# Norm roots as exp(-0.5 ln) on ScalarE instead of a power on GpSimd, and another rule for which products go to GpSimd

## The chip, the cores and the metric

The kernel runs on one core of one Trainium2 chip. The metric is device time in microseconds of one execution; the time before is the median of three runs, 29434.43 us (29426.01 to 29453.37). The engines are named as the profile names them: PE is TensorE, DVE is VectorE, ACT is ScalarE, POOL is GpSimd, SP issues all DMAs.

## What is computed

Eight images of 64 channels and 128 x 128 pixels, in fp32, pass a softmax-weighted 3x3 filter (layer 0) and then a block that holds a two-layer, two-directional state-space scan and a gated feed-forward (layer 1). Cut to what matters here:

```python
def layernorm(x, w, b):                      # rmsnorm: the same without the mean
    mu = x.mean(-1, keepdims=True)
    var = ((x - mu) ** 2).mean(-1, keepdims=True)
    return (x - mu) * jax.lax.rsqrt(var + EPS) * w + b

def selective_scan(u, dt, A, Bm, Cm, D, z):
    dt = jax.nn.softplus(dt)
    dA = jnp.exp(jnp.einsum('bdl,dn->bldn', dt, A))
    dBu = jnp.einsum('bdl,bnl,bdl->bldn', dt, Bm, u)
    # hs[l] = dA[l] * hs[l-1] + dBu[l], along l = 128*128 tokens
    y = jnp.einsum('bldn,bnl->bdl', hs, Cm) + D[None, :, None] * u
    return y * jax.nn.silu(z)

x_norm = ln4d(input, norm1_w, norm1_b)       # over the 64 channels
seq = layernorm(tokens(x_norm), pe_norm_w, pe_norm_b)
for i in range(2):                           # two directions in each
    seq = bimamba_block(seq, ...)            # begins with an rmsnorm
x = input + dw * x_mamba                     # dw: 1x1 and depthwise 3x3 of x_norm
xn = ln4d(x, norm2_w, norm2_b)
g1, g2 = split(depthwise3x3(ffn_in @ xn))
return x + ffn_out @ (jax.nn.gelu(g1, approximate=False) * g2)
```

The scan has 128 channels x 16 states per direction, so it is by far the largest part.

## The kernel before

**Tiling.** The scans of all images, layers and directions are cut into 512 chunks of 1024 tokens (64 per image: 16 for each of two directions in each of two layers). A chunk has 16 *units* (U); a unit is one tile of 128 (channel, state) pairs by 1024 tokens. Units go in pairs k, whose order is in `PAIRS`.

**One unit.** `decay` (L1112) makes w = exp(dt * A) on ScalarE into one of two PSUM buffers. `drive` (L1107) makes bu = dt*u*B on GpSimd, 2048 columns for a pair, in three buffers. `scan` (L1122) runs the recurrence on VectorE. `product` (L1151) multiplies by C, either on GpSimd or on VectorE. `keep` (L1148) copies the last column to `state` on ScalarE. `collect` (L1162) adds over states on PE, once per pair, and gives the pair's hs buffer (one of three) free. Where the product is made is decided by `on_pool` (L1095): if it is GpSimd, the scan writes to hs in SBUF and the product follows one unit later; if it is VectorE, the scan writes in place into w and the product reads it from there.

```python
def on_pool(self, u):
    if u % 2 or u % 8 == 4 or self.t0 + u - 1 in gelu_times:
        return False
    return u != 8 or self.beside_front or self.beside_gelu
```

**Order.** There is no scheduler at run time: `at(time, phase, fn)` (L396) files every step under a time, counted in units, and one of six phases (FEED, SCAN, MID, PROD, DECAY, REST), and the program is written out in that order, each engine keeping it. Chunk i has its scans at times 16i to 16i+15; its projections come up to two chunks earlier, its norm (second direction only) in the chunk after.

**Background stages.** Beside the scans of one image, other steps run on the same engines: *fronts* of the next image (`Front.plan`, L648: filter, three norms n1, n2, n3, every 24 units), *mix* of the image before (`Mix.plan`, L752: two 3x3 convolutions and one norm, every 13 units) and *feed-forward* of the image before (`Ffn.plan`, L912: three GELUs every 24 units). In a cycle of 64 chunks, mix lies beside chunks 0 to 11 (it starts beside chunk 62), feed-forward beside 12 to 34, fronts beside 36 to 63. Image 0 has its own first fronts partly ahead of all scans (a prologue of 514 us) and then beside its first 12 chunks; no mix or feed-forward runs beside image 0. Image 7 has no fronts beside it, and its own mix starts beside its chunk 51; its own feed-forward stands alone after the last scan.

**A norm.** `means` (L469) sums squares on PE into PSUM, 8 columns. `means_out` (L473) copies them to `r` on ScalarE and adds eps. `root` (L477) raises `r` to the power -0.5 on GpSimd. `spread` (L480) broadcasts the roots over the channels on PE into a bank `rb`, which VectorE multiplies by (L609, L641, L1221). Each step has its own time in `plan`: in Front, `means_out` of n1 and `root` stand at a + 26, `spread` at a + 28, the multiplication at a + 29.

**Tables.** [...] `silu` (L1012), `softplus` (L1039) and `gelus` (L868) each use a set of their own; `decay` and the softmax use Exp. Loads of tables are put in by the compiler just ahead of the instruction that needs them, so the load back stands at L1117, ahead of the next decay.

Of the kernel before, what the change touches and what calls it, by code (L numbers as in the profile page):

```python
# [10 lines left out]
AF = mybir.ActivationFunctionType  # L11
ALU = mybir.AluOpType
# [3 lines left out]
P = 128  # L16
# [3 lines left out]
ROWS = 4  # L20
# [14 lines left out]
U = G * G  # L35
PW = W + 2
FEED, SCAN, MID, PROD, DECAY, REST = range(6)
# [18 lines left out]
def kernel(ctx: ExitStack, tc: tile.TileContext, a: dict, out: bass.AP):  # L56
# [6 lines left out]
    nc = tc.nc  # L63
    x = a["x"]
    B = x.shape[0]

    def row(v):
        return v.rearrange("(c o) -> c o", o=1)

# [2 lines left out]
    def const(shape, name, dt=F32):  # L72
        return wp.tile(shape, dt, tag=name, name=name)
# [38 lines left out]
    nc.vector.tensor_tensor(center, center, ident, ALU.add)  # L112
    eps = const([P, 1], "eps")
    nc.vector.memset(eps, EPS)
    neg_half = const([P, 2 * ROWS], "neg_half")
    nc.vector.memset(neg_half, -0.5)

    sel_y = const([P, 32, 1], "sel_y")
    nc.vector.tensor_reduce(sel_y, ident.rearrange("k (m n) -> k m n", n=G), AX.X, ALU.add)
# [71 lines left out]
    with tc.tile_pool(name="wspill", bufs=1) as fp, tc.tile_pool(name="wprep", bufs=2) as pp, \  # L191
            tc.tile_pool(name="wps", bufs=4, space=PSUM) as pps:
        with tc.manual_schedule():
# [23 lines left out]
            def by_taps(rows, taps, n, k):  # L217
# [6 lines left out]
                )  # L224
                return t[0:n]

            w1n = pp.tile([32, C * 9], F32, tag="w1n", name="w1n")
            nc.sync.dma_start(w1n, a["L0_conv_w1"].rearrange("o c i j -> o (c i j)"))
            resn = pp.tile([C, C * 9], F32, tag="resn", name="resn")
# [15 lines left out]
            for part in ((0, 0, 0, P), (1, 0, HID, P), (2, 0, HID + P, REST_HID), (2, C, P, REST_HID)):  # L245
                _, _, r0, n = part
# [38 lines left out]
            t = turned(outn[:, P:HID], ident[0:C, 0:C], REST_HID, C)  # L285
            for h in range(2):
                nc.scalar.copy(wout_b[C * h : C * h + REST_HID, :], t[0:REST_HID, 0:C])
            for (g, c0, r0, n), fn, fdn in parts:
# [7 lines left out]
                for k in range(9):  # L296
                    i, j = divmod(k, 3)
                    t = turned(fn2[:, k, :], ident[0:n, 0:n], P, n)
# [21 lines left out]
            for l in range(DEPTH):  # L320
# [8 lines left out]
                t = turned(twice(inz, DI, C)[:, 0, :], ident, P, DI)  # L329
# [8 lines left out]
                for d in range(2):  # L338
# [3 lines left out]
                    for j in range(KC):  # L342
                        t = turned(taps[:, j, :], ident, P, DI)
                        at = j if d == 0 else KC - 1 - j
# [6 lines left out]
                    t = turned(xbc, ident[0:32, 0:32], DI, 32)  # L351
# [9 lines left out]
                    for g in range(G):  # L361
                        t = turned(sel_d[:, g, :], al, P, DS)
# [33 lines left out]
    def at(time, phase, fn, *args):  # L396
        steps.setdefault((time, phase), []).append((fn, args))
# [65 lines left out]
    class Norm:  # L463
# [8 lines left out]

        def means_out(self):  # L473
            self.r = wk.tile([P, 2 * ROWS], F32, tag="r", name="r", bufs=4)
            nc.scalar.activation(self.r, self.mp[:, 0 : 2 * ROWS], AF.Identity, bias=eps)  # L475

        def root(self):  # L477
            nc.gpsimd.tensor_tensor(self.r, self.r, neg_half, ALU.pow)  # L478

        def spread(self, ps):  # L480
            self.rb = ps("rb")
# [15 lines left out]
    class Front:  # L497
# [150 lines left out]
        def plan(self, a):  # L648
            n1, n2, n3 = self.n1, self.n2, self.n3
            b = a - FRONT_STEP  # L650
            self.alone = a + FRONT_STEP < -2
            at(b - 5, REST, self.load_xa)
            for i in range(3):
                at(b + 1 + i, REST, self.hidden, i)
            at(b + 6, DECAY, self.hidden_out)
            at(b + 21, REST, self.logits)
            at(b + 23, DECAY, self.less_max)
            at(b + 23, DECAY, self.exps)
            at(b + 24, DECAY, self.sums)
            at(b + 24, REST, self.softmax)  # L660
            for i in range(3):
                at(b + 26 + 2 * i, DECAY, self.piece, i)
                if i < 2:
                    at(b + 27 + 2 * i, REST, self.less_piece, i)
            at(b + 31, REST, self.turn)
            at(b + 32, DECAY, self.turned)
            at(a + 6, REST, self.load_xb)
            for k in range(9):

                t = a + k + (k >= 3)  # L670
                at(t + 11, REST, self.weight, k)
                at(t + 12, DECAY, self.weighted, k)
                at(t + 13, REST, self.gather, k)
            at(a + 23, DECAY, self.filtered)
            at(a + 23, REST, self.store_x1)
            at(a + 23, REST, self.centered, acc_tile, "x1")
            at(a + 24, DECAY, self.centered_out)
            at(a + 25, REST, lambda: n1.means(bg_tile, self.sq))
            at(a + 26, DECAY, n1.means_out)
            at(a + 26, REST, n1.root)  # L680
            at(a + 28, REST, n1.spread, bg_tile)
            at(a + 29, DECAY, self.scaled, n1)
            at(a + 29, DECAY, self.first_norm)
            at(a + 30, REST, self.pointwise)
            at(a + 31, DECAY, self.pointwise_out)
            at(a + 31, REST, self.store_rows, dw_img[self.p], "dwt")
            at(a + 31, REST, self.centered, acc_tile, "xn")
            at(a + 32, DECAY, self.centered_out)
            at(a + 33, REST, lambda: n2.means(acc_tile, self.sq))
            at(a + 34, DECAY, n2.means_out)  # L690
            at(a + 34, REST, n2.root)
            at(a + 36, REST, n2.spread, acc_tile)
            at(a + 37, DECAY, self.scaled, n2)
            at(a + 37, DECAY, self.second_norm)
            at(a + 37, REST, self.store_h)
            at(a + 38, REST, lambda: n3.means(bg_tile, self.sq))
            at(a + 39, DECAY, n3.means_out)
            at(a + 39, REST, n3.root)
            at(a + 47, REST, n3.spread, bg_tile)
            at(a + 48, DECAY, self.third_norm)  # L700
            at(a + 48, REST, self.store_hn)
# [9 lines left out]
    class Mix(Front):  # L711
# [40 lines left out]
        def plan(self, a):  # L752
            n1 = self.n1
            for h in range(2):
                at(a - 6 + h, REST, self.load_conv, dw_img[self.p], "dww", h)
                at(a - 4 + h, REST, self.load_conv, xm_img, "xmw", h)
            at(a - 1, REST, self.load_h)
            for i in range(3):
                at(a + i, REST, self.conv, 0, "dww", i)
                at(a + 3 + i, REST, self.conv, 1, "xmw", i)  # L760
            at(a + 3, DECAY, self.branch_out)
            at(a + 2, REST, self.load_x1)
            at(a + 5, REST, self.add_h)
            at(a + 8, DECAY, self.times)
            at(a + 8, REST, self.plus)
            at(a + 10, REST, self.store_x2)
            at(a + 10, REST, self.centered, bg_tile, "x1")
            at(a + 11, DECAY, self.centered_out)
            at(a + 12, REST, lambda: n1.means(bg_tile, self.sq))
            at(a + 13, DECAY, n1.means_out)  # L770
            at(a + 13, REST, n1.root)
            at(a + 16, REST, n1.spread, bg_tile)
            at(a + 17, DECAY, self.scaled, n1)
            at(a + 17, DECAY, self.norm)
            at(a + 17, REST, self.store_rows, xn_img, "hc")
# [7 lines left out]
    class Ffn:  # L783
# [84 lines left out]
        def gelus(self):  # L868
            if self.alone:
                nc.scalar.activation(self.gt, self.gt, AF.Gelu)  # L870
            else:
                self.gt = tmp("gt")
                nc.scalar.activation(self.gt, self.rest[0], AF.Gelu)
            for h in range(2):
                nc.scalar.activation(self.ga[h], self.ga[h], AF.Gelu)

        def rest_times(self):
            nc.vector.tensor_tensor(self.gt, self.gt, self.rest[1], ALU.mult)
# [66 lines left out]
    gelu_times = {IMAGE * b + FFN_AT + FFN_STEP * c + GELU for b in range(B - 1) for c in range(NCH)}  # L945
# [7 lines left out]
    class Chunk:  # L953


        def __init__(self, i):
            self.b, self.l, self.d, self.t, self.second = order[i]
            self.i, self.t0 = i, U * i
            self.first = i % NT == 0
            self.pairs = PAIRS[i % 2]  # L960
            r, last = self.t0 % IMAGE, self.b == B - 1
            self.beside_front = (
                FRONT_AT - FRONT_STEP <= r < FRONT_AT + NCH * FRONT_STEP + 16 and not last
            ) or self.t0 < FIRST_FRONT_AT + NCH * FRONT_STEP + 16
            self.beside_gelu = any(self.t0 - U <= t < self.t0 + 2 * U for t in gelu_times)
            self.prev = None
            self.bus, self.hss, self.ws = {}, {}, {}
            self.dup, self.dtp, self.bp, self.cp, self.yv = {}, {}, {}, {}, {}
            self.norm = Norm()
# [42 lines left out]
        def silu(self):  # L1012
            nc.scalar.activation(self.xc, self.xc, AF.Silu)
            if self.second:
                nc.scalar.activation(self.gt, self.gt, AF.Silu)

        def store_gate(self):
            self.gt_d = sd.tile([DI, T], F32, tag="gate", name="gate_dram", bufs=4)
# [20 lines left out]
        def softplus(self):  # L1039
            dt = self.dt  # L1040
            nc.scalar.activation(dt, dt, AF.Softplus)

        def bc(self):
            self.bcp = mm_tile("bcp")
# [50 lines left out]
        def on_pool(self, u):  # L1095


            if u % 2 or u % 8 == 4 or self.t0 + u - 1 in gelu_times:
                return False
            return u != 8 or self.beside_front or self.beside_gelu  # L1100

        def over_pair(self, what, k):
            j = self.pairs[k][0]
# [132 lines left out]
        def plan(self):  # L1236
# [21 lines left out]
            b = self.t0  # L1258
# [41 lines left out]
                at(b + 7, REST, self.store_h)  # L1300
            feed(b + 12, lambda: n.means(mm_tile, self.sq))
            at(b + 13, DECAY, n.means_out)
            at(b + 14, REST, n.root)
            feed(b + 17, n.spread, mm_tile)
            at(b + 18, DECAY, self.normed)
            if self.l:
# [51 lines left out]
```

## Time and profile before

| | us |
|---|---|
| median of the runs | 29434.43 |
| runs | 29426.01 to 29453.37 |
| span of the profiled execution | 29479.5 |
| first scan starts, in the profile | 514.2 |
| last scan ends | 29033.0 |

The prediction works with the profiled execution, whose span is 45 us longer than the median. A row of a group reads: line, engine, operation, output<-input with sizes, count | busy us, mean ns of one | idle time of the engine ahead of them, and what ended most of it. A row of waits reads: who <- for whom: us in total, times, longest. In a table of stretches, each row gives the stretch, its length, and each engine's busy time and instructions in it. Busy time of a stretch is a union, so neighbours that overlap are counted once, while the mean duration of a group is that of one instruction by itself.

The ends of the two stages that have no scans are small: the prologue holds 22 of the 768 roots, the 447 us after the last scan 5.

### The profile page before, as it was taken

The numbers are of one execution on the slowest core, as the hardware profiler recorded it, in microseconds if no ns is written. First come the engines' busy times: TensorE is split into PE (matmuls) and PEld (weight loads), VectorE is DVE, ScalarE is ACT, GpSimd is POOL, SyncE is SP. The second block draws the span as 40 slices with busy tenths as digits, with TensorE's granted clock in tenths as the row PEclk, the third lists the DMA queues.
The fourth block names the chain that finished last, engine by engine and source line by source line (L and its number), as shares of the span: only waits on it lengthen the run. The fifth ranks groups of instructions, "written<-read, shape, count | busy, mean of one in ns | idle before, by whom it ended". The sixth has DMA issues, their size and how long they took to land. (4 is left out here: it accounts for less than half of the span.)

```text
span 29479.5 us, 312296 instructions
## 1 busy us (share of the span) xinstructions
PE 23358.6 (79%) x97708; PEld 7341.1 (25%) x97708; DVE 27316.3 (93%) x17567; ACT 18561.4 (63%) x28361; POOL 27648.1 (94%) x8732
## 2 busy tenths in 40 slices
PE   6666888878788787887878778787787877878678
PEld 3211222223222232222322223222222222222123
DVE  4999999999999999999999999999999999999997
ACT  3666666666666666666666666666666666666663
POOL 3999999999999999999999999999999999999994
PEclk7777888988889888988888888898888988889789
DMA  5776777767777678776787767777677776777674
GB/s 121 225 244 215 229 249 242 235 216 234 252 234 236 218 230 255 236 232 216 238 251 235 231 220 236 252 238 230 220 241 248 239 224 222 243 245 238 217 249 142
DMA packets 2592280, 6762.81 MB, mean 229 GB/s; under 512 B 431270, under 2 KB 736822, under 8 KB 2589462
## 3 DMA queue, kind: packets, MB, share of 16 engines
q1 hardware_dynamic: 2590614, 6742.83, 71.4%
q8 instruction: 773, 12.66, 0.2%
q14 instruction: 893, 7.32, 0.1%
HBM read 5509.49 MB, written 1265.19 MB: 230 GB/s over the span
## 5 line engine op out<-in xcount | busy, mean ns | idle before, releaser
L1109 POOL TENSOR_TENSOR bu<-dup,bp 128x2048 f32<-128x2048 f32 x4096 | 18564.5, 4537 | 370.7 <-DVE w L1137 238.3
L1117 ACT ACTIVATE w<-dtp,a_neg 128x1024 f32<-128x1024 f32 x8192 | 9159.6, 1118 | 800.4 <-DVE hs L1135 341.3
L1156 POOL TENSOR_TENSOR hs<-hs,cp 128x1024 f32<-128x1024 f32 x2832 | 6678.4, 2358 | 250.2 <-ACT state L1149 191.9
L1159 DVE TENSOR_TENSOR hs<-w,cp 128x1024 f32<-128x1024 f32 x5360 | 6562.7, 1224 | 361.7 <-DMA cp<-bc_dram 132.8
L1137 DVE TENSOR_TENSOR_SCAN w<-w,state,bu 128x1024 f32<-128x1024 f32 x2683 | 6290.4, 2345 | 292.8 <-ACT w L1117 291.9
L1135 DVE TENSOR_TENSOR_SCAN w<-w,state,bu 128x1024 f32<-128x1024 f32 x2677 | 6278.7, 2345 | 243.6 <-ACT w L1117 241.3
L1175 PE MATMUL y<-hs,sel_y 128*32 128x512 f32 x32768 | 5121.8, 700 | 60.6 <-POOL hs L1156 60.3
L1149 ACT COPY state<-w 128x1 f32<-128x1 f32 x5360 | 837.9, 156 | 5524.7 <-DVE hs L1159 5474.4
L1137 DVE TENSOR_TENSOR_SCAN hs<-w,state,bu 128x1024 f32<-128x1024 f32 x1413 | 3308.2, 2341 | 209.9 <-issue 121.7
L1135 DVE TENSOR_TENSOR_SCAN hs<-w,state,bu 128x1024 f32<-128x1024 f32 x1419 | 3321.0, 2340 | 41.3 <-ACT state L1149 16.7
L1168 PE MATMUL y<-xc,dskip 128*64 128x512 f32 x4096 | 1577.5, 860 | 1660.6 <-ACT yv L1192 1392.1
L987 PE MATMUL xp<-hn,wx 128*128 128x512 f32 x4096 | 2350.5, 703 | 669.3 <-ACT xc L993 469.2
L819 PE MATMUL fp<-fw,bgw 128*128 128x512 f32 (+1 forms) x5760 | 2270.0, 637 | 104.6 <-ACT ga L866 71.7
L1149 ACT COPY state<-hs 128x1 f32<-128x1 f32 x2832 | 541.4, 191 | 1968.6 <-DVE hs L1137 1018.6
L1175 PEld LDWEIGHTS y<-hs,sel_y 128*32 128x32 f32 x32768 | 729.8, 117 | 3676.1 <-issue 2444.1
L1028 PE MATMUL dp<-xc,wdt 128*128 128x512 f32 x2048 | 1237.5, 688 | 462.1 <-ACT dt L1035 362.6
L478 POOL TENSOR_TENSOR r<-r,neg_half 128x8 f32<-128x8 f32 x768 | 1262.6, 1644 | 300.7 <-ACT r L475 279.2
L1117 ACT ACT_TABLE_LOAD x1134 | 1454.9, 1283 | 20.0
L1065 POOL TENSOR_TENSOR dt<-dt,xc 128x1024 f32<-128x1024 f32 x512 | 1211.2, 2366 | 221.8 <-DMA dt_dram<-dt 187.7
L825 PE MATMUL fp<-fw,bgw 64*128 64x512 f32 (+1 forms) x5760 | 1415.3, 610 | 0.0
L589 PE MATMUL acc<-t,ident 128*128 128x512 f32 x2160 | 1265.5, 669 | 85.6 <-DVE hc L609 84.7
L987 PEld LDWEIGHTS xp<-hn,wx 128*128 128x128 f32 x4096 | 830.8, 216 | 1988.2 <-issue 964.3
(214 smaller groups left out, 25747.8 us busy)
## 6 DMA issues: line engine op xcount, KB each, us to landing
bp<-bc_dram SPq DMA_DIRECT2D x4096, 256.0 KB, 4.2
dup<-du_dram SPq DMA_DIRECT2D x4096, 256.0 KB, 5.0
dtp<-dt_dram SPq DMA_DIRECT2D x4096, 256.0 KB, 5.0
cp<-bc_dram SPq DMA_DIRECT2D x4096, 256.0 KB, 5.0
hn<-hn_dram SPq DMA_DIRECT2D x1024, 256.5 KB, 4.9
dt_dram<-dt SPq DMA_DIRECT2D x512, 512.0 KB, 3.4
du_dram<-dt SPq DMA_DIRECT2D x512, 512.0 KB, 2.6
yf_dram<-yv SPq DMA_DIRECT2D x512, 256.0 KB, 4.7
```

What stands on the lines that cost most here:

```text
L819: nc.tensor.matmul(o, wpair[:, i, g, m], self.win[h][:, i : i + ROWS, 0:W], start=(i == 0), stop=False)
L825: nc.tensor.matmul(o, wlast[rows, i, g, m], self.win[h][rows, i : i + ROWS, lo : W + lo], start=False, stop=(i == 2),)
L987: nc.tensor.matmul(self.xp[h], wx[:, self.l, self.d, i, :], self.hn2[:, s.start + 2 * i : s.stop + 2 * i], start=(i == 0), stop=(i == 1),)
L1109: nc.gpsimd.tensor_tensor(bu, self.dup[self.pairs[k][1]], self.over_pair("bp", k), ALU.mult)
L1117: nc.scalar.activation(w, self.dtp[gp][:, i, :], AF.Exp, scale=a_neg[:, self.l, self.d, g, j : j + 1])
L1135: nc.vector.tensor_tensor_scan(to, w, bu, s0, ALU.mult, ALU.add)
L1137: nc.vector.tensor_tensor_scan(to[:, ::-1], w[:, ::-1], bu[:, ::-1], s0, ALU.mult, ALU.add)
L1149: nc.scalar.copy(self.column(u), h[:, T - 1 : T] if self.d == 0 else h[:, 0:1])
L1156: nc.gpsimd.tensor_tensor(hs, hs, c, ALU.mult)
L1159: nc.vector.tensor_tensor(hs, w, c, ALU.mult)
L1168: nc.tensor.matmul(self.y[C * h : C * h + C, :], dskip[:, self.l, self.d, C * gp : C * gp + C], self.xc[:, s], start=True, stop=False,)
L1175: nc.tensor.matmul(self.y[lo : lo + 32, :], sel_y, hs[:, i, s], start=False, stop=(k % 4 == 3))
```

## The change

1. `means_out` applies Ln, with eps as its bias, where it applied Identity, and then Exp with scale -0.5 in place on `r`. `root` and its constant `neg_half` are gone, and so is GpSimd's part in every norm.
2. `logs_and_exps` loads by name a set of tables that holds both functions: once at the start, and after `silu`, `softplus` and (with scans beside it) `gelus`.
3. `spread` moves one unit earlier in three of five places.
4. `on_pool` has another rule: of the even units, 0, 2, 6, 8, 10 and 14 go to GpSimd in every chunk, and unit 9 in odd chunks, each unless a GELU stands one unit before (for unit 9: at the chunk's time 7).

```diff
+    def logs_and_exps():
+        nc.scalar.preload_act_table_set("natural_log_exp_and_others")
...
-    neg_half = const([P, 2 * ROWS], "neg_half")
-    nc.vector.memset(neg_half, -0.5)
...
+            logs_and_exps()
             w1n = pp.tile([32, C * 9], F32, tag="w1n", name="w1n")
...
             self.r = wk.tile([P, 2 * ROWS], F32, tag="r", name="r", bufs=4)
-            nc.scalar.activation(self.r, self.mp[:, 0 : 2 * ROWS], AF.Identity, bias=eps)
-
-        def root(self):
-            nc.gpsimd.tensor_tensor(self.r, self.r, neg_half, ALU.pow)
+            nc.scalar.activation(self.r, self.mp[:, 0 : 2 * ROWS], AF.Ln, bias=eps)
+            nc.scalar.activation(self.r, self.r, AF.Exp, scale=-0.5)
...
             at(a + 26, DECAY, n1.means_out)
-            at(a + 26, REST, n1.root)
-            at(a + 28, REST, n1.spread, bg_tile)
+            at(a + 27, REST, n1.spread, bg_tile)
...
             at(a + 34, DECAY, n2.means_out)
-            at(a + 34, REST, n2.root)
-            at(a + 36, REST, n2.spread, acc_tile)
+            at(a + 35, REST, n2.spread, acc_tile)
...
             at(a + 39, DECAY, n3.means_out)
-            at(a + 39, REST, n3.root)
...
             at(a + 13, DECAY, n1.means_out)
-            at(a + 13, REST, n1.root)
-            at(a + 16, REST, n1.spread, bg_tile)
+            at(a + 15, REST, n1.spread, bg_tile)
...
                 nc.scalar.activation(self.ga[h], self.ga[h], AF.Gelu)
+            if not self.alone:
+                logs_and_exps()
...
-            self.beside_gelu = any(self.t0 - U <= t < self.t0 + 2 * U for t in gelu_times)
...
                 nc.scalar.activation(self.gt, self.gt, AF.Silu)
+            logs_and_exps()
...
             nc.scalar.activation(dt, dt, AF.Softplus)
+            logs_and_exps()
...
-            if u % 2 or u % 8 == 4 or self.t0 + u - 1 in gelu_times:
-                return False
-            return u != 8 or self.beside_front or self.beside_gelu
+            if u == 9:
+                return self.i % 2 == 1 and self.t0 + 7 not in gelu_times
+            return u % 2 == 0 and u % 8 != 4 and self.t0 + u - 1 not in gelu_times
...
             at(b + 13, DECAY, n.means_out)
-            at(b + 14, REST, n.root)
             feed(b + 17, n.spread, mm_tile)
```

## The prediction, made before the changed kernel was run

> **What bounds the kernel now.** I read the engine totals first, then the groups, then one table of stretches, because the totals mix stages with different limits.
>
> ```profile
> span 29479.5 us, 312296 instructions
> PE 23358.6 (79%) x97708; PEld 7341.1 (25%) x97708; DVE 27316.3 (93%) x17567; ACT 18561.4 (63%) x28361; POOL 27648.1 (94%) x8732
> ...
> L1109 POOL TENSOR_TENSOR bu<-dup,bp 128x2048 f32<-128x2048 f32 x4096 | 18564.5, 4537 | 370.7 <-DVE w L1137 238.3
> ...
> L1156 POOL TENSOR_TENSOR hs<-hs,cp 128x1024 f32<-128x1024 f32 x2832 | 6678.4, 2358 | 250.2 <-ACT state L1149 191.9
> L1159 DVE TENSOR_TENSOR hs<-w,cp 128x1024 f32<-128x1024 f32 x5360 | 6562.7, 1224 | 361.7 <-DMA cp<-bc_dram 132.8
> ...
> L1149 ACT COPY state<-w 128x1 f32<-128x1 f32 x5360 | 837.9, 156 | 5524.7 <-DVE hs L1159 5474.4
> ...
> L478 POOL TENSOR_TENSOR r<-r,neg_half 128x8 f32<-128x8 f32 x768 | 1262.6, 1644 | 300.7 <-ACT r L475 279.2
> L1117 ACT ACT_TABLE_LOAD x1134 | 1454.9, 1283 | 20.0
> ```
>
> VectorE and GpSimd are both nearly full, ScalarE is not: its state copies alone sat 5474 us behind VectorE. A product costs 2.36 us on GpSimd and 1.22 on VectorE; a root of 8 columns costs 1.64 on GpSimd. The timeline shows neighbours overlapping, so what one more or one less is worth is 2.32, 1.17 and 1.60 us.
>
> The table of stretches (us, then busy us and instructions of PE, PEld, DVE, ACT, POOL, then clock, DMA share, GB/s) shows which engine is full where:
>
> ```profile
> 0.00:514.00 514.00, 312.68 (x1306) 173.55 (x1306) 153.40 (x354) 95.42 (x222) 57.70 (x63) 0.67 0.45 82
> 514.00:1198.00 684.00, 515.24 (x2178) 170.71 (x2178) 644.89 (x437) 434.31 (x689) 671.84 (x228) 0.82 0.69 220
> 1198.00:2350.00 1152.00, 720.37 (x2660) 195.85 (x2660) 1123.38 (x646) 723.25 (x1063) 1126.68 (x328) 0.75 0.72 237
> 7665.00:8311.00 646.00, 504.44 (x2200) 135.46 (x2200) 614.41 (x354) 412.15 (x616) 638.34 (x199) 0.87 0.80 253
> 8311.00:9524.00 1213.00, 1048.31 (x4139) 315.88 (x4136) 1141.34 (x682) 798.01 (x1171) 1146.24 (x333) 0.90 0.71 235
> 9689.00:10317.00 628.00, 476.54 (x2003) 152.11 (x1999) 589.10 (x403) 397.46 (x632) 615.31 (x211) 0.83 0.66 215
> 10317.00:11252.00 935.00, 781.86 (x3535) 280.70 (x3527) 878.71 (x608) 609.88 (x973) 911.76 (x311) 0.88 0.74 237
> 27465.00:28382.00 917.00, 527.37 (x1849) 121.76 (x1847) 899.17 (x498) 582.39 (x841) 901.13 (x256) 0.72 0.65 220
> 28382.00:29033.00 651.00, 548.22 (x2433) 163.79 (x2432) 633.47 (x384) 415.72 (x636) 640.95 (x202) 0.88 0.82 260
> ```
>
> The lines are: prologue; image 0 beside its own fronts; image 0 calm; then image 2 beside mix (chunks 0 to 11), beside feed-forward (12 to 33), beside early fronts (37 to 47), beside late fronts (48 to 63); image 7 calm; image 7 beside its own mix. GpSimd is full (97.5 to 99%) beside mix and fronts. Beside feed-forward both stand at 94%; there GpSimd's waits are mostly for VectorE (29 us for a bu buffer), so VectorE leads. In calm stretches both stand at 98%. In the late fronts VectorE's idle time has these owners:
>
> ```profile
> DVE w L1135 <- ACT w L1117: 17.5, 14, 3.2
> DVE hn L1221 <- PE rb L484: 14.8, 5, 4.8
> ...
> DVE hn L641 <- PE rb L484: 9.2, 5, 2.1
> DVE hc L609 <- PE rb L484: 5.1, 5, 2.4
> ```
>
> 29 us of the 56 idle are waits for a norm's spread (rb), which waits for a root queued on GpSimd.
>
> **The parts.**
>
> *Roots off GpSimd.* 768 x 1.644 = 1263 us leave GpSimd. By stretch (the same table for L478 alone): 24, 18, 15, 16, 19, 46, 3, 24 roots in the order above after the prologue, and 22 in it.
>
> *Logarithm and exponential on ScalarE.* The logarithm takes the place of the Identity that moved the mean out (262 ns, median), at the same size and with the same bias: nothing. The exponential is new, 768 times, and waits for the logarithm just ahead of it. Nearest row, that Identity: 0.26 us, some 200 us in all. Queued behind it on ScalarE are decays, which VectorE's next scan but one waits for; the 5474 us of idle time cover it. From both sides: nothing, or all 200 us where the cover is gone; I take nothing.
>
> *Table loads.* The Trainium skill, "ScalarE: Activation LUTs", The hidden batching unit, puts exp and ln in one set, and under What ACT_TABLE_LOAD costs asks about 2.66 us for a switch, drain included. The row says 1.283 us, and the 1134 loads had 20 us of idle time ahead of them in all, so no drain shows. Were each root to switch away and back, ScalarE would get 768 x 2 x 1.283 = 1971 us by the row and 4086 by the page (an estimate), both too much. But the instruction order of the changed program has 2274 loads against 2273 before, so neither sum is due. Each return load moves ahead of one state copy. It gains only where ScalarE idled between: walking the trace, late scans directly behind a load lost 194 us, but only 1 us of that had idle time to give. Bounds 0 and -194; I take 0.
>
> *Spread one unit earlier.* In Front (twice) and Mix it stands one unit sooner on PE. No DMA and no SP entry moves. It takes its PSUM bank a unit earlier; queued behind it are the y matmuls of the next collect, so a late exponential would hold them. PE already waited 485 us for roots on GpSimd, so I expect less waiting, not more, and take nothing by itself; the rb waits go.
>
> *Products.* Counting by the rule of `on_pool`, GpSimd gets 3188 products instead of 2832: unit 8 everywhere unless a GELU forbids it, and unit 9 in 228 odd chunks. GpSimd +356 x 2.32, VectorE -356 x 1.17. The Trainium skill speaks against this: "GPSIMD Engine Reference", Elementwise, keeps "use DVE for elementwise" as the rule, at a ratio of 1.96. The rows agree on the ratio (2358/1224 = 1.93). By the rule the exchange loses 826 - 417 = 409 us of engine time; by the table only the fuller engine of each stretch counts. Without the products, early fronts would have GpSimd at 585 and VectorE at 589, balanced already. With them (+6) it is 599 and 582, so there the rule is right. In late fronts (+9) it is 859 and 868, where the products help by 10 us. So most of the gain is the roots'; beside mix and in calm stretches the products cost.
>
> **The sum**, busy time of the fuller engine divided by the share it reaches now, unless said:
> - Mix: POOL 638.3 + 16 x 2.32 - 15 x 1.60 = 651.4, at 98.8%: 659, +13. Seven images: **+91**.
> - Feed-forward: DVE 1141.3 - 7 x 1.17 = 1133.1 at 94.1%: 1204, -9. Seven: **-63**. (POOL 1136.8.) The scans behind GELU lose 17 us here, unchanged.
> - Early fronts: POOL 615.3 + 13.9 - 30.4 = 598.8 at 98.0%: 611, -17. Seven: **-119**.
> - Late fronts: POOL 911.8 + 20.9 - 73.6 = 859.1, DVE 868.2; DVE becomes the bound. Its 56 idle without the 29 of rb would give 895; two equally full engines wait for each other, so I take 900, -35. Seven: **-245**.
> - Image 0 beside its fronts: POOL 671.8 + 13.9 - 38.4 = 647.3 at 98.2%: **-25**. Image 0 calm: +32 products, POOL 1172.1 at 98.5%: **+38**.
> - Image 7 calm: +26 products, -3 roots, POOL 956.6 at 98.5%: **+54**. Its last stretch: +18, -24: **+3**.
> - Prologue: some 14 of its 22 roots lie on a serial chain (n1, then n2), each shorter by 1.64 - 0.26: **-20**. Tail, 5 roots: **-4**.
>
> Together -290 us. The profiled span is 45 us above the median 29434.4 of the runs shown; I take the difference over to the median: **29144, predicted 29140**.
>
> **Rivals.**
> 1. *More than that.* The relief pays in full: 403 us off GpSimd (768 x 1.60 less 356 x 2.32), 417 off VectorE, and waits go too. Late fronts at 887, feed-forward 1192, early fronts 604, mix +9: -572 in all, 28862. For it: calm stretches run at 98% now. Against: beside feed-forward neither engine gets there.
> 2. *The fronts are held by something else.* PE is at 84% there, and 17.5 us are late decays. With early fronts -7, late -12, feed-forward 0, mix +13, the rest as above: +4 and the span about stands, 29440; with mix +19 and feed-forward +7, +150.
> 3. *Slower: three products in a row.* In odd chunks units 8, 9 and 10 all go to GpSimd. From unit 7 it gets product, drive, product, drive, product: 3 x 2.32 + 2 x 4.49 = 15.9 us until unit 9's is done. Unit 14's scan takes over that pair's hs buffer and VectorE reaches it after 7 scans of 2.345 and 4 products, 21 us. Of the 5 us between, the pair's y matmuls (4 x 0.70, row of L1175) take 2.8, so some 2 us remain for what unit 5 left over. From a backlog of 2 us at unit 7 the scan waits, up to 2.3 us in each of 228 chunks: +524 - 290 = +234, 29670. For it: in stretches where GpSimd is full a backlog is the normal state. Against: there its time is already counted in the sum; it is only dear where VectorE leads.
> 4. *The sets are not shared at run time*, +1971 us on ScalarE: the load count excludes it.
>
> **Numbers.** Forecast (-150 to -410) 0.48; rival 1 0.17; rival 2 0.16, of which 0.07 is still a gain; rival 3 and costs of both signs unnamed 0.19. A measurement of this kernel tells about 0.2% (59 us) from no change. Faster 0.72, same 0.09, slower 0.19. The range leaves out the far ends of rivals 1 and 3: 28900 to 29500; the forecast's own is 29025 to 29285.
>
> **What would show it.** Right: no POOL row for r; POOL near 27225 busy (27648 - 1263 + 840), DVE near 26880 (27316 - 436); the windows of fronts shorter, mix and calm ones longer by 13 and some 40 to 55 us; rb waits of VectorE mostly gone; table loads near 2274. Wrong: VectorE waiting for PE y or POOL bu at unit 14 of odd chunks (rival 3), late decays growing by the exponentials' 200 us, or late fronts unchanged with both engines idle (rival 2).

## The result and the profile after

The changed kernel took 29517.38 us (29504.08 to 29529.85, nine runs) against 29434.43 us of the kernel before in the same comparison: a ratio of 1.003, interval 1.0021 to 1.004. It is slower, by 83 us, where 290 us of gain were forecast, and lies 17 us above the top of the stated range.

The page of the changed kernel, totals and the rows that answer to those shown of before:

```profile
span 29512.3 us, 311865 instructions
PE 23365.9 (79%) x97708; PEld 7281.0 (25%) x97708; DVE 26912.6 (91%) x17210; ACT 18733.8 (63%) x29130; POOL 27249.6 (92%) x8320
...
L1155 POOL TENSOR_TENSOR hs<-hs,cp 128x1024 f32<-128x1024 f32 x3188 | 7539.5, 2369 | 336.6 <-ACT state L1148 258.3
L1158 DVE TENSOR_TENSOR hs<-w,cp 128x1024 f32<-128x1024 f32 x5004 | 6127.7, 1225 | 377.9 <-DMA cp<-bc_dram 165.1
...
L1148 ACT COPY state<-w 128x1 f32<-128x1 f32 x5004 | 792.8, 158 | 4891.0 <-DVE hs L1158 4839.0
...
L68 ACT ACT_TABLE_LOAD x1137 | 1458.8, 1283 | 20.9 <-PEq L1345 0.7
```

The change did what it says. No row on GpSimd writes r any more, the products are the 3188 that were counted, the table loads are as many as before, and both full engines lost about what was forecast: GpSimd stands at 27250 us (27225 expected), VectorE at 26913 (26880). Some 400 us of work left each of the two fullest engines, and the time rose. So the question is where that relief went.

The table of stretches of the changed kernel, with the columns as before: image 2 beside mix, feed-forward, early fronts, late fronts, then image 7 calm:

```profile
7670.00:8324.00 654.00, 503.10 (x2189) 132.67 (x2188) 596.08 (x338) 411.22 (x628) 654.00 (x201) 0.87 0.79 253
8324.00:9534.00 1210.00, 1040.44 (x4155) 313.10 (x4155) 1134.94 (x676) 806.93 (x1190) 1134.42 (x324) 0.92 0.70 234
9696.00:10325.00 629.00, 468.35 (x2010) 151.01 (x2009) 581.22 (x394) 400.69 (x648) 602.05 (x198) 0.85 0.67 217
10325.00:11257.00 932.00, 784.13 (x3532) 279.20 (x3531) 868.76 (x602) 619.61 (x1021) 857.56 (x273) 0.88 0.73 236
27468.00:28424.00 956.00, 546.14 (x1848) 114.21 (x1847) 871.80 (x474) 581.80 (x844) 956.00 (x280) 0.70 0.62 210
```

Read the busy columns against the length. Late fronts: GpSimd 858 (859.1 forecast) and VectorE 869 (868.2 forecast), both 63 to 74 us short of the 932 that the stretch still takes; it took 935. Early fronts: 602 and 581 of 629, which were 628. Neither engine fills these stretches. In the calm stretch and beside mix GpSimd is busy for 956.00 of 956.00 and 654.00 of 654.00: in this kernel a GpSimd that sets the pace stands at 100%, and not at the 97.5 to 99% of before.

What the added products hold up there shows in the row of PE's matmuls of y, which read hs after the product, before and after:

```profile
L1175 PE MATMUL y<-hs,sel_y 128*32 128x512 f32 x32768 | 5121.8, 700 | 60.6 <-POOL hs L1156 60.3
```
```profile
L1174 PE MATMUL y<-hs,sel_y 128*32 128x512 f32 x32768 | 5226.3, 698 | 644.5 <-POOL hs L1155 643.3
```

PE stood still for products of GpSimd for 643 us (60 before, and 19 in the run with the roots alone, below): 255 us of it beside mix, 237 in the calm stretches, 103 in chunks 34 to 36, and only 48 beside the fronts. VectorE's scans waited 179 us for y (53 before). 108 us of that stand at unit 14 of odd chunks, the sign that the prediction had given for its rival 3; in the fronts there are none. Beside mix of image 2, where no scan had waited for y before:

```profile
DVE hs L1134 <- PE y L1174: 14.0, 7, 4.0
```

VectorE's waits in the late fronts of the changed kernel (who <- for whom: us, times, longest):

```profile
DVE w L1134 <- ACT w L1116: 23.2, 15, 4.4
DVE hn L1220 <- PE rb L484: 19.0, 5, 4.8
...
DVE hn L641 <- PE rb L484: 5.7, 4, 1.9
DVE t L578 <- PE wb L574: 5.0, 8, 1.1
...
DVE hc L609 <- PE rb L484: 1.9, 1, 1.9
```

The waits for rb, which were to go with the roots, are 26.6 us (19.0 + 5.7 + 1.9); they were 29.1. One of them, on ScalarE, PE and then VectorE, in the order of time (start, us, what, and in brackets the idle time ahead and who ended it):

```profile
10492.11 0.21 ACT L478 ACTIVATE r<-r 128x8 f32<-128x8 f32 x1
...
10500.96 0.67 ACT L521 ACTIVATE ha<-hp,b 64x512 f32<-64x512 f32 x1
```
```profile
10501.68 2.07 PE L618 MATMUL dwp<-hc,bgw 128*128 128x512 f32 x2 [3.33 <-ACT ha L521]
10503.68 1.92 PE L1045 MATMUL bcp<-xc,wbc 128*32 128x512 f32 x4
10506.87 2.08 PE L601 MATMUL cp<-hc,center 128*128 128x512 f32 x2 [1.26 <-ACT state L1148]
10508.88 0.52 PE L560 MATMUL tp<-identb,sp 128*54 128x128 bf16 x3
10509.09 0.47 PE L484 MATMUL rb<-ident,r 128*64 128x128 f32 x1
...
10509.29 1.66 PE L484 MATMUL rb<-ident,r 128*64 128x128 f32 x15
```
```profile
10504.07 2.34 DVE L1134 TENSOR_TENSOR_SCAN hs<-w,state,bu 128x1024 f32<-128x1024 f32 x1
10511.01 0.69 DVE L1220 TENSOR_TENSOR hn<-h,rb 128x512 f32<-128x512 f32 x1 [4.60 <-PE rb L484]
```

ScalarE had written the roots by 10492.3. The spread came 17 us later. Most of that is its place in the plan, some four units after the root (a unit takes 3.6 us here), but PE had also stood still for 3.33 us ahead of dwp, the pointwise matmul of one front chunk, until ScalarE had written ha (L521), and what stands behind dwp in PE's queue waited with it. dwp does not read ha. Both use the one bank `acc`: `hidden_out` of a later front chunk has to read hp out of it before dwp may overwrite it, and `hidden_out` stands in the same time unit as `pointwise`, behind a decay and other steps of ScalarE. The rows of dwp over the whole trace, before and after:

```profile
L618 PE MATMUL dwp<-hc,bgw 128*128 128x512 f32 x256 | 219.4, 952 | 410.9 <-ACT ha L521 409.0 <-ACT hc L613 1.9
```
```profile
L618 PE MATMUL dwp<-hc,bgw 128*128 128x512 f32 x256 | 222.8, 967 | 368.9 <-ACT ha L521 368.9
```

The waits for ha are in 112 places, 14 of the 16 front chunks of each image (7 of them lie in the prologue, ahead of all scans). The same stop makes decays late: behind dwp stands xp, which ScalarE's xc waits for, and behind xc the next decay (one scan lost 3.50 us so at 10421.6).

### The profile page after: what moved, and what is told of

The parts are those of the page before. It is cut to its first block, busy times and chain, and to the rows that moved or that the text cites. A ratio compares the mean times of both kernels' runs of the same rounds, so it can differ in the third digit from the quotient of the medians.

```text
span 29512.3 us, 311865 instructions
## 1 busy us (share of the span) xinstructions
PE 23365.9 (79%) x97708; PEld 7281.0 (25%) x97708; DVE 26912.6 (91%) x17210; ACT 18733.8 (63%) x29130; POOL 27249.6 (92%) x8320
## 5 line engine op out<-in xcount | busy, mean ns | idle before, releaser
L1108 POOL TENSOR_TENSOR bu<-dup,bp 128x2048 f32<-128x2048 f32 x4096 | 18602.6, 4547 | 538.9 <-DVE w L1136 285.0
L1155 POOL TENSOR_TENSOR hs<-hs,cp 128x1024 f32<-128x1024 f32 x3188 | 7539.5, 2369 | 336.6 <-ACT state L1148 258.3
L1158 DVE TENSOR_TENSOR hs<-w,cp 128x1024 f32<-128x1024 f32 x5004 | 6127.7, 1225 | 377.9 <-DMA cp<-bc_dram 165.1
L1136 DVE TENSOR_TENSOR_SCAN w<-w,state,bu 128x1024 f32<-128x1024 f32 x2544 | 5964.8, 2345 | 270.5 <-ACT w L1116 264.5
L1134 DVE TENSOR_TENSOR_SCAN w<-w,state,bu 128x1024 f32<-128x1024 f32 x2460 | 5770.9, 2346 | 350.6 <-ACT w L1116 341.1
L1174 PE MATMUL y<-hs,sel_y 128*32 128x512 f32 x32768 | 5226.3, 698 | 644.5 <-POOL hs L1155 643.3
L1134 DVE TENSOR_TENSOR_SCAN hs<-w,state,bu 128x1024 f32<-128x1024 f32 x1636 | 3814.2, 2340 | 191.7 <-PE y L1174 96.6
L1136 DVE TENSOR_TENSOR_SCAN hs<-w,state,bu 128x1024 f32<-128x1024 f32 x1552 | 3621.1, 2341 | 327.3 <-issue 152.1
L984 PE MATMUL xp<-hn,wx 128*128 128x512 f32 x4096 | 2285.9, 686 | 396.7 <-ACT xc L990 247.0
L1148 ACT COPY state<-hs 128x1 f32<-128x1 f32 x3188 | 607.4, 191 | 2091.5 <-DVE hs L1136 1076.9
L990 ACT ACTIVATE xc<-xp,cbias 128x512 f32<-128x512 f32 x1024 | 695.7, 679 | 969.7 <-PE xp L984 967.3
```

What stands on the lines that cost most here:

```text
L984: nc.tensor.matmul(self.xp[h], wx[:, self.l, self.d, i, :], self.hn2[:, s.start + 2 * i : s.stop + 2 * i], start=(i == 0), stop=(i == 1),)
L1108: nc.gpsimd.tensor_tensor(bu, self.dup[self.pairs[k][1]], self.over_pair("bp", k), ALU.mult)
L1134: nc.vector.tensor_tensor_scan(to, w, bu, s0, ALU.mult, ALU.add)
L1136: nc.vector.tensor_tensor_scan(to[:, ::-1], w[:, ::-1], bu[:, ::-1], s0, ALU.mult, ALU.add)
L1155: nc.gpsimd.tensor_tensor(hs, hs, c, ALU.mult)
L1158: nc.vector.tensor_tensor(hs, w, c, ALU.mult)
```

## The experiments

All are compared with the kernel before, on one chip each time. Theory A is that of the prediction; theory B says that beside the fronts the time is VectorE's work plus these stops between PE and ScalarE.

**Roots alone.** The changed kernel with the old `on_pool`:

```diff
-            if u == 9:
-                return self.i % 2 == 1 and self.t0 + 7 not in gelu_times
-            return u % 2 == 0 and u % 8 != 4 and self.t0 + u - 1 not in gelu_times
+            if u % 2 or u % 8 == 4 or self.t0 + u - 1 in gelu_times:
+                return False
+            return u != 8 or self.beside_front or self.beside_gelu
```

> The changed kernel with the old rule for products: roots on ScalarE, 2832 products on GpSimd. Theory A (as predicted: GpSimd is the bound beside the fronts, and VectorE's waits for rb are waits for roots queued on it): late fronts -29 us, early fronts -8, mix -13 per image, prologue and tail -24, in all some -370 us against the kernel before, 29060 us. Theory B (beside the fronts the time is VectorE's busy time plus stalls of a chain between PE and ScalarE, and GpSimd only looks full): fronts unchanged within 5 us per image, mix -8 per image, prologue and tail -24, in all -60 to -110 us, about 29350 us. In B the rb waits stay near 25 us in a late-fronts window.

Measured: 29356.20 us, 0.9975 (0.9963 to 0.9986), 72 us less than before. Its stretches beside mix and late fronts:

```profile
7625.00:8268.00 643.00, 500.39 (x2204) 136.55 (x2200) 614.30 (x354) 413.20 (x630) 617.89 (x184) 0.87 0.80 257
...
10270.00:11198.00 928.00, 774.82 (x3532) 278.22 (x3531) 878.83 (x610) 619.69 (x1020) 841.62 (x266) 0.89 0.74 238
```

In the late fronts GpSimd lost 70 us of work (911.8 to 841.6) and the stretch 7; beside mix it lost 20 and the stretch 3. VectorE's waits for rb there are 20.8 us. This is theory B's figure. A GpSimd at 97.5 or 98.8% was not what held these stretches.

**Products alone.** The kernel before with the new `on_pool` (the diff above, the other way round, without the roots).

> The kernel before with the new rule for products: powers on GpSimd, 3188 products there. Theory A: every stretch pays its products on GpSimd (2.32 us each) as far as it is full, mix +35, feed-forward +10, early fronts +14, late fronts +20 per image, calm stretches +60 and +60, in all some +700 us against before, 30130 us. Theory B: mix +30 per image and calm stretches +50 each as in A, but fronts only +10 to +15 in all per image: +450 to +550 us, about 29930 us. Both: much dearer alone than together with the roots, and fewer late decays at unit 11 of odd chunks do not show in the time.

Measured: 29850.86 us, 1.0144 (1.013 to 1.0158), 422 us more than before, nearer to B and still below its range. Beside mix, in image 2:

```profile
7765.00:8444.00 679.00, 514.79 (x2184) 136.84 (x2182) 595.45 (x337) 409.82 (x613) 679.00 (x217) 0.86 0.77 243
8444.00:9644.00 1200.00, 1042.04 (x4160) 313.76 (x4157) 1134.42 (x677) 798.97 (x1174) 1159.08 (x339) 0.92 0.71 236
```

Beside mix GpSimd is at 100% and the stretch 33 us longer. Beside feed-forward GpSimd has more work than before (1159 against 1146) and the stretch is 13 us shorter: VectorE leads there. The parts do not add up: -72 and +422 make +350, together they cost 83, which fits with the products moving into the place that the roots leave on GpSimd.

**The stop between PE and ScalarE, taken away.** The changed kernel, and one line:

```diff
-            at(b + 6, DECAY, self.hidden_out)
+            at(b + 4, DECAY, self.hidden_out)
```

> The changed kernel with hidden_out of a front chunk two units earlier (time b + 4 instead of b + 6), so that ScalarE has read the bank that the pointwise matmul of another front chunk takes over; nothing else is changed. Theory A: PE's waits are not on the path; within 25 us of the changed kernel, 29517 us. Theory B: PE's 369 us of waits of dwp for ha go, and with them late decays and late rb beside late fronts: 1.5 to 3 us for each of 112 front chunks beside scans, -170 to -330 us against the changed kernel, 29190 to 29350 us, and the late-fronts window of image 2 falls from 932 us to 895 to 915.

Measured: 29291.39 us, 0.9954 (0.9941 to 0.9966), 226 us less than the changed kernel. PE's waits for ha ahead of dwp are gone:

```profile
L618 PE MATMUL dwp<-hc,bgw 128*128 128x512 f32 x256 | 153.2, 682 | 20.3 <-ACT hc L613 20.2
```

Late fronts of image 2:

```profile
10235.00:11141.00 906.00, 771.62 (x3529) 275.77 (x3522) 868.49 (x603) 618.77 (x1020) 856.37 (x273) 0.90 0.75 242
```
```profile
DVE hn L1220 <- PE rb L484: 8.3, 4, 4.2
DVE hn L641 <- PE rb L484: 7.6, 3, 2.9
...
DVE w L1134 <- ACT w L1116: 7.0, 12, 1.2
...
DVE hc L609 <- PE rb L484: 0.7, 1, 0.7
```

With the same work on both engines the stretch is 26 us shorter, late decays are down from 23.2 to 7.0 us and rb waits from 26.6 to 16.6. Theory B holds for the late fronts: no instruction was added or left out, only one step moved. PE was also quicker: dwp took 682 ns in the mean instead of 967, and PE was busy for 771.62 us of the stretch at a granted clock of 0.90, after 784.13 us at 0.88. Whether the higher clock only follows from the stop being gone, or is a part of the gain by itself, no run separates.

In the early fronts the move brought little: 37 us over seven images by the start times of the chunks, against 172 in the late ones. In image 2 the stretch went from 629 to 625 us; VectorE's waits for late decays fell from 14.4 to 3.9 us there, but those for wb rose from 7.2 to 12.6 and those for rb from 9.5 to 12.3. In the longest wait for wb, 3.97 us at 9660.4, PE had stood 2.85 us for a GpSimd product ahead of y; what sets the others is open.

**Roots and the moved step, and the moved step alone.** The first and third edits together, and the third edit on the kernel before.

> Roots on ScalarE, the old rule for products, and hidden_out two units earlier: the first and the third experiment together. Theory B: the two gains add, since one lies beside mix and in the prologue, the other beside late fronts: late fronts of image 2 at 910 to 920 us (VectorE 879 busy, some 37 idle as in the third experiment), 29356 - 185 = about 29170 us, 29130 to 29220. Theory A (GpSimd was the bound and its relief only hidden by chance): no more than 20 us below 29356.

> The kernel before with hidden_out two units earlier alone: powers stay on GpSimd, old rule. Theory B alone (GpSimd never led beside the fronts): the same gain as in the third experiment, late fronts -27 us per image, about -200 us, 29230 us. Theory B with a second limit just behind it (GpSimd, 912 of 935 us busy in the late fronts of image 2, comes next): late fronts stop at 912/0.985 = 926 us, -9 per image, early fronts 0, prologue -14: -80 us in all, 29350 us; then the removal of roots pays there only once the stall is gone.

Measured: 29235.24 us together, 0.9936 (0.9923 to 0.9948), and 29253.06 us for the moved step alone, 0.9942 (0.993 to 0.9955). The moved step brings 174 us without any root leaving GpSimd; with it in place the roots bring 18 more, where they brought 72 without it. The two were expected to add up further (29170): the first is a miss by 65 us. The second lies between its two branches. Its late fronts:

```profile
10222.00:11144.00 922.00, 775.92 (x3535) 278.26 (x3527) 879.05 (x609) 609.97 (x972) 911.89 (x311) 0.89 0.74 240
```

GpSimd, with its powers, is busy for 911.9 of 922 us, so the second limit shows here, close to the 926 expected of it; with the roots gone the same stretch takes 911. By the start times of the chunks 81 us of the profiled gain (239 us) lie in the late fronts, 64 in the early ones, 29 in chunks 34 to 36 and 26 in the prologue; the second branch had 63, nothing, nothing and 14 there. With the roots gone too the late fronts give 70 us more, and early fronts, feed-forward and prologue take 80 back. What does that was not tried.

**The exponential's price.** The changed kernel with one instruction in `means_out`, so that a norm multiplies by another function of the variance:

```diff
-            nc.scalar.activation(self.r, self.mp[:, 0 : 2 * ROWS], AF.Ln, bias=eps)
-            nc.scalar.activation(self.r, self.r, AF.Exp, scale=-0.5)
+            nc.scalar.activation(self.r, self.mp[:, 0 : 2 * ROWS], AF.Exp, scale=-0.5)
```

> The changed kernel without the logarithm: means_out is one exponential straight from PSUM, so a norm multiplies by exp(-0.5(v + 0)) and has one ScalarE instruction fewer, 768 in all, some 200 us of ScalarE. If the added instruction is hidden (taken at nothing in the prediction): within 20 us of the changed kernel, 29517 us. If it is what ate the gain beside the fronts, by late decays: -100 to -200 us, 29320 to 29420 us, and the late decays of a late-fronts window fall from 23.5 us to below 18.

Measured: 29502.52 us, 1.0027 (1.0017 to 1.0037), 15 us below the changed kernel, whose nine runs spread over 26. The late decays fell only from 23.2 to 20.7 us. The second instruction, 209 ns long and 160 us in all, is hidden as forecast; it did not eat the gain.

**Products only where VectorE leads.** The fourth kernel (roots and the moved step) with a rule by stage, ahead of the old one; 2992 products are on GpSimd, 160 of the 356 that the change had added:

```diff
+            if u == 9 and self.i % 2 and (self.beside_front or self.beside_gelu):
+                return self.t0 + 7 not in gelu_times
             if u % 2 or u % 8 == 4 or self.t0 + u - 1 in gelu_times:
                 return False
             return u != 8 or self.beside_front or self.beside_gelu
```

> As the fourth, with unit 9 of odd chunks on GpSimd only beside fronts and beside feed-forward, where VectorE leads; beside mix and in calm stretches the old rule. Theory B: late fronts of image 2 as in the third experiment, 906 us, mix as in the first, 643 us, calm of image 7 917 us: 60 to 110 us less than the fourth, about 29080 us. If three products in a row make scans wait there, no less than the fourth.

Measured: 29128.87 us, 0.99 (0.9886 to 0.9913), 106 us less than the fourth and 298 less than before, the fastest kernel here. Late fronts, feed-forward and mix:

```profile
7563.00:8208.00 645.00, 499.13 (x2201) 136.44 (x2201) 613.13 (x353) 413.48 (x630) 616.46 (x184) 0.88 0.80 255
8208.00:9415.00 1207.00, 1042.27 (x4147) 315.42 (x4143) 1134.29 (x676) 806.97 (x1189) 1133.45 (x323) 0.92 0.71 235
...
10199.00:11104.00 905.00, 766.65 (x3534) 272.00 (x3535) 870.82 (x605) 618.82 (x1020) 857.38 (x273) 0.91 0.75 244
```

The 905 us of the late fronts against 911 in the fourth, with three products in a row, refute rival 3 for these stretches; VectorE's scans waited 0.7 us for y in the late fronts of all images.

**The same rule with hidden_out left where it was**, the changed kernel with products by stage:

> The changed kernel with its new rule for unit 9 only beside fronts and feed-forward, and the old rule beside mix and in calm stretches; hidden_out stays at b + 6. If the changed kernel is slower only because of the products added where GpSimd is full (mix +11 against the old rule in each of 7 images, calm stretches +35 and +15, the end of image 7's scans), this gives them back: 29310 to 29370 us, at least 140 us below the changed kernel, with late fronts still at 925 to 935 us. If the products beside the fronts cost as well (three in a row), it stays above 29400 us.

Measured: 29365.12 us, 0.9981 (0.9972 to 0.999), 152 us less than the changed kernel. Beside mix in image 2 and in the calm stretch of image 7 GpSimd has its gaps again, and the stretches are 638 and 915 us, after 654 and 956:

```profile
7636.00:8274.00 638.00, 495.60 (x2195) 135.70 (x2196) 612.83 (x354) 414.07 (x630) 615.79 (x184) 0.88 0.81 258
27350.00:28265.00 915.00, 510.44 (x1851) 116.03 (x1850) 898.52 (x498) 583.69 (x844) 900.80 (x256) 0.75 0.65 219
```

So the products beside mix and in calm stretches account for the loss of the change, and more. Against roots alone (29356) the products by stage bring nothing while the stop is there, and 106 us once it is gone.

## Why the prediction was wrong

By its own steps, in us over all images; measured is from the start times of the chunks in the two profiles:

| step | forecast | measured |
|---|---|---|
| prologue and tail | -24 | -23 |
| image 0 beside its fronts | -25 | +1 |
| image 0 calm | +38 | +13 |
| mix, 7 images | +91 | +48 |
| feed-forward, 7 images | -63 | -27 |
| chunks 34 to 36 | 0 | -18 |
| early fronts, 7 images | -119 | +26 |
| late fronts, 7 images | -245 | -20 |
| image 7 calm, and its last stretch | +57 | +34 |

The measured ones make +34 with rounding, as do the two spans (29479.5 to 29512.3); the medians differ by 83. The profiled execution of before was 45 us above its own median and that of after 5 us below, so the column is 50 us too favourable to the change in all; in which rows is not known.

- **The step that failed is the reading of the fronts**: "GpSimd is full (97.5 to 99%) beside mix and fronts", and from it busy time divided by the share it reached. 389 us of gain were put on stretches of fronts (25 + 119 + 245); these came out 7 us longer (+1 + 26 - 20). The runs show in its place, for the late fronts: VectorE's work plus the stops of a chain from ScalarE's ha through PE's dwp to the next decay or spread (moving one step took 172 us off them over seven images, with the work of both engines as it was). GpSimd's 912 us came close to the 935 of the stretch, as a second limit at 922. In the early fronts this chain explains only a part. Of what is new there, 19 us are waits of scans for a GpSimd product in chunk 37, the first of the stretch (up to 3.6 us in each image, none before); the rest of the 26 us that they grew is open.
- "29 us of the 56 idle are waits for a norm's spread (rb), which waits for a root queued on GpSimd" is the same error in small: 26.6 of the 29.1 us stayed with no root on GpSimd. These waits name PE, and what PE had stood for was in part dwp's bank: 10 of the 26.6 us went with the moved step, and what holds the other 16.6 is open. The row of dwp's waits for ha, 409 us in the trace of before, was there to be read; the prediction used only VectorE's and GpSimd's waits and one sum of PE's for roots.
- The late fronts' 900 us took VectorE as the bound with the rb waits gone and the other waits as they were. Instead they rose: late decays from 17.5 to 23.2, wb from 0.2 to 5.0. One scan, lost 2.19 us to a late decay before and 3.50 after, with a product of VectorE less ahead of it: where the decay comes at a fixed time, a faster VectorE waits longer for it.
- Right were the counts of products and loads, the relief of both engines, the price of the exponential, and that products cost beside mix and in calm stretches. The prologue's -23 for -24 is partly luck: in the runs with the roots on ScalarE the prologue alone came out between -6 and -33 us, and the moved step alone gave it -26. Those costs of products were too high, since GpSimd reached 100% and not the 98.5 or 98.8% that they were divided by (956 us for the calm stretch of image 7 where 971 were forecast). The 98.5% is also not what the calm stretches reached before: by the table it is 97.8% in image 0 and 98.3% in image 7.
- Rival 2 had the mechanism ("the fronts are held by something else", with PE and late decays named) and, with +4 to +150, the measured +83. The number is partly luck: it had -7 us for early fronts and +13 for mix in each image, and +4 and +7 were measured; by its own terms its upper end is +95 (-49 - 84 + 133 + 49 + 46), not +150. (Rival 1's named terms, with the rest as in the sum, make -542, not -572.) Rival 2 was given 0.16 because its evidence was an engine total, PE at 84%, and not a chain.
- Rival 3's waits are there, but not where it held them dear: scans wait for y at unit 14 of odd chunks beside mix and in calm stretches, where GpSimd is full. That is how the cost of a full GpSimd reaches VectorE, and the sum had it already as GpSimd's busy time; in the fronts no scan waited for y.

The change is slower, then, because its gain and its cost lie in different stretches: the roots' relief falls mostly on fronts, where GpSimd did not set the pace, and the added products also on calm stretches and mix, where they bring it to 100%.

## What to carry to other kernels

An engine that is 97 or 98% busy in a stretch need not set its pace: ask what the other engines' waits are, and follow a wait past the engine that it names to what that engine's queue was stopped by. A shared PSUM bank whose reader and next writer stand in the same step stops what stands behind the writer in its engine's queue, and moving the reader earlier is cheaper to try than moving work between full engines. Work should be moved to an engine by the stretch, not by one rule for the whole kernel, and here it paid only after the stop that both engines wait for was gone.

## What was not expected

- A GpSimd that sets the pace shows no gap at all here: 956.00 of 956.00 us, 654.00 of 654.00, 679.00 of 679.00.
- With 356 more products on GpSimd PE's idle time ahead of y grew by 583 us; VectorE's scans waited 126 us longer for y.
- GpSimd's rows grew a little as its load changed: a product from 2358 to 2369 ns, a drive from 4537 to 4547 ns in the mean. What causes it was not tried.
- Two changes that bring 72 and 174 us apart bring 191 together, and products worth nothing (+9) before the stop was removed bring 106 after it.
